# Two of four w_down blocks prepared from the copy that was loaded to measure them

## The chip, the cores and the metric

The kernel runs on one core of a Trainium2 chip. The core has five engines that each work through their own list of instructions in order and wait for one another by semaphores: TensorE (PE; its weight loads are shown as PEld), VectorE (DVE), ScalarE (ACT), GpSimd (POOL) and SyncE (SP). Here every DMA is issued by SP, so SP's list is also the order in which transfers start. The metric is the device time of one execution in microseconds.

## The reference

The input x has 4 batches of 2048 rows of 512 numbers. The block computes a cross-attention and then a feed-forward network whose operands are rounded to FP4 in blocks of 16:

```python
x = x + xattn(layernorm(x), ctx, ctx, mask, Wq, bq, Wk, bk, Wv, bv, Wo, bo)   # 16 heads of 32, 77 keys
x = x + ffn(layernorm(x), w_gate, w_up, w_down)

def fp4_quant_dequant(x):              # blocks of 16 along the last dimension
    scale = max(max(abs(block)) / 6, 1e-12)
    idx = searchsorted(MID, abs(block / scale))
    return GRID[idx] * sign(block) * scale

gate = fp4(x) @ fp4(w_gate).T          # w_gate, w_up: 1408 x 512
y    = fp4(x) @ fp4(w_up).T
h    = silu(gate) * y
out  = fp4(h) @ fp4(w_down).T          # w_down: 512 x 1408
```

So the three feed-forward weights have to be quantized and transposed on the chip before the first tile can use them. The kernel holds each quantized weight as two 16-bit parts (a high and a low one) with a common power of two, and that power comes from the largest absolute value of the whole matrix.

## The kernel before

The 8192 rows of x are worked through in 64 tiles of 128 rows. For a tile t the steps are: load x (xin), layernorm, transposition by DMA (xT), the product with Wq (qps), transposition (qst), scores (scps), maximum on DVE (mx), its negative on POOL (nmx), exponentials on ACT (line 944), the split into two parts (ph), transposition (pT), the product with the values (avps), normalization (an, ahl), transposition (aT), the product with Wo (ops), the residual sum (x, line 1004), the second layernorm, quantization and transposition (xqT), gate and up products (gps, ups), silu and product (hh), quantization (hqhl), transposition (hT), the down product (dps) and the store. Several tiles are in flight at once, so each engine's list interleaves steps of neighbouring tiles.

**The order of issue is written out.** Each piece of work is a Python generator that yields `step(engine, take, give, wait, fire)` and then emits its instructions. `take` and `give` name buffers of a ring (a buffer that is taken must have been given back by an earlier holder), `wait` and `fire` name events. The class Order (line 113) goes through a written list, INTRO (line 26), in which a word such as `wd0*2` means "two steps of the chain wd0"; then through 3013 steps that are chosen by the due times in PLACE (line 88), and last through OUTRO. Take, give, wait and fire don't make the chip wait: they only say which orders are allowed. What waits on the chip follows from the order of the instructions and the semaphores between them.

**The weights.** Before the first tile can go through the network, the kernel prepares w_gate, w_up and w_down in four blocks each. A block of w_down is 128 rows of 1408 numbers, 704 KB. Two functions deal with it:

- `down_max` (line 746; the word `ad` in INTRO) loads a block (tile name wmraw) into one of two buffers and takes the largest absolute value of every 16 numbers on DVE (wamd, line 377). Blocks 0 and 2 use the buffer hT, blocks 1 and 3 the buffer hqhl; both have one copy. The buffer is given back after the maximum, so the four blocks go 0, 1, 2, 3, two at a time. Then `weight_scale(2)` finds the largest value of the matrix.
- `weight_put(2, i)` (line 787; the words `wd0` to `wd3`) prepares block i. Its steps are: the reciprocal of the scales on DVE (rh, lines 763 and 764); a second load of the block into the same kind of buffer (tile name wraw); a multiply on POOL (line 704); the absolute value on ACT (wa, line 810); the rounding, two instructions on DVE (lines 710 and 711); the spread of the two parts of the scales on ACT (line 715, twice, from shh and slh, which `weight_scales`, line 775 and the words `sd`, makes); a multiply on DVE (line 719); and a DMA transposition into wdT (line 822), after which the buffer is given back.

So w_down is loaded twice. The second loads of blocks 0 and 1 are issued when the maxima are done, those of blocks 2 and 3 when block 0 has left hT and block 1 has left hqhl. The buffers hT and hqhl are later the ones that the down product of each tile uses, and `scales_h` (line 1053) waits until all four blocks are in wdT.

Other words of INTRO that matter below are `x.t` (residual, line 863: a load of x on SP, and the sum with the bias on POOL, line 869), `at.t` (attention, line 871), `kb` and `vb` (keys and values of the next batch).

Of the kernel before, what the change touches and what calls it, by code (L numbers as in the profile page):

```python
# [7 lines left out]
F32 = mybir.dt.float32  # L8
# [15 lines left out]
AHEAD = 14  # L24
PASSES = ((0, 0), (0, 1), (1, 0))
INTRO = (
    "lg*2 ck ag v wg0*3 ag sg lu au lu*3 wu0*3 au*2 wu2 au*4 wu1 wu3 au*3 wu2 wu0 wg0 o su*4 lk*6 mask wu1 lk ck*6 lk "
    "ck*3 lk*4 q*2 wu0 lg*2 ag*8 lo v lo v lo v lo*4 v*4 o*2 wu0 sg*2 ck*5 dc v q*4 wg2 su*2 lo o lo*2 o*2 wg0 su*2 "
    "sg at.0*3 pc0*4 dk pk1*2 v*3 dv pv2*2 pv1*2 pv2*2 pk1*2 at.1*3 pv0*2 wg0 wu2 wu1*2 pv3*2 pv1*2 lk q*2 dq pk3*3 "
    "wu0 wg2 at.0*3 at.2 wu2 pv0*2 pc1*2 wu1*2 pv3*2 pk3 pc1*2 pk0*2 sg*3 pk2*2 pc2*4 pk2*2 wg1 o*2 wg0 wu3 pk0*2 "  # L30
    "pq1*2 k pq3 kp pads pq3 pq1*2 pq3*2 o kp k*2 o*2 do mv wg3 su wu2 wu1 wg3 at.2 pq0*2 kp k kp k wu2*2 wg3*2 wg2 "
    "sg*2 pq2*2 at.2 at.1*3 at.3 pq0*2 vp mv vp mv pq2*2 po2 po0 po2*2 po0 po2 at.0 k*2 sg*3 wg3 wg2 wg3 k*4 wg2*2 "
    "wg1*2 wg3 wg2 ad wg1 po1*2 at.0*3 vp mv at.2*3 at.4 k*3 vp vp1 mv*2 vp2 vp3 x.0 wg1 at.3*2 po0*2 mv*5 vp2 vp3 "
    "vp1 ad sd ad wd0 po3*2 po1*2 vp3 wg1 k*2 at.3*2 at.5 at.1 at.3 at.1*2 ad wd1 ad keep po3*2 pads k*9 wu3 at.4 k*2 "
    "ad wd2 ad vp0 su*3 at.4*3 k0 at.5*2 vp0*2 v0*2 e0 v0*2 x.1*2 e0*2 v0 e0 v0 e0 v0*2 e0*2 v0 e0 ad wd0 ad*2 wd1 "
    "wu3 k0 f0 k0 f0 k0 f0 k0 f0 at.0*4 at.1 v0 e0 v0 e0 at.0 at.6*2 wg1 ad wd0*2 wd3 wd0 at.0 at.2 at.4 at.2*2 x.0 "
    "vp1 keep x.2 vp2 keep*2 x.3*2 ad*3 at.0*4 at.1 at.0 at.2 at.5*2 at.7 sd*3 wd0 at.1 at.0 at.1 wd0*2 wd2 at.0 wu3 "
    "at.7 wu3 at.3 at.5 sd*2 at.1*7 at.2 at.1 at.6 at.0*3 at.3*2 at.0 x.4 at.2*2 at.3 wd1*3 wd2*3 wu3 sd*2 at.6*2 "
    "at.8 at.2*2 wd1 sd wd2 sd*2 wd1*2 at.0 at.7 at.4 at.6 at.0*2 r.0 at.1*5 wd2*2 at.0*2 wd3 sd at.2*5 at.3 at.2 "
    "px.0*2 at.4*2 at.0*3 at.7*2 px.0 at.0 wd3*2 at.1 at.3 at.2 at.3*2 at.1*2 r.1 at.0 gu.0 at.8 at.9*2 at.1*2 x.2 "  # L40
    "at.3*3 at.2*2 at.4 at.5*2 at.7 wd3 gu.0*3 at.2*3 at.5 at.1 px.1*2 at.1 at.3*4 wd3*2 at.1*2 at.4 at.5 s.0 gu.0 "
    "h.0 gu.0 s.0 h.0 px.1 at.1*2 wd3 at.2*2 r.2 at.4 at.2*5 at.3*3 at.6 gu.1*2 at.4 px.2*3 at.4 at.3*3 at.2*3 s.0 "
    "gu.1 h.0 gu.1 h.0 ph.0*3 h.0 at.3*2 r.3 at.8 at.4*7 at.6*2 at.5 at.6 at.3*3 s.1 h.1 s.1 h.1 gu.2*4 at.5*2 ph.0*2 "
    "at.8*3 s.2 h.0*5 h.2 at.4*2 at.3*3 px.3*2 at.5*8 at.7*3 px.3 at.3 at.10 at.4*3 gu.1*2 s.1 h.1*4 at.3 s.2 h.2 h.1 "
    "at.6*2 at.7 at.6*7 x.4 ph.1*5 h.1 h.0*3 at.10 at.5 at.4*4 r.4 at.6*2 at.5*4 at.4*3 at.9 x.5 gu.2*2 s.2 h.2 "
    "at.8*3 h.1*2 gu.3 s.3 at.9 at.7*6 at.8 px.4*3 at.9*2 at.11 h.2 ph.2 h.2*2 gu.3 h.3 gu.3*2 at.6*4 at.4*4 ph.2 "
    "at.5 at.6 at.7*5 s.3 h.3 h.2 ph.2*2 x.5 at.5*3 h.2 h.1*3 r.5 at.11 at.5*3 at.10 x.6 gu.3 s.3 gu.3 h.3 at.9*3 "
    "ph.2 h.2*2 gu.4 s.4 at.10 at.8*6 at.9 px.5*3 at.10*2 at.12 h.3 ph.3 h.3*2 gu.4 h.4 gu.4*2 at.7*4 at.5*4 ph.3 "
    "at.6 at.7 at.8*5 s.4 h.4 h.3 ph.3*2 x.6 at.6*3 h.3 h.2*3 vb.16*2 r.6 at.12 at.6*3 at.11 x.7 gu.4*2 s.4 h.4 "
    "at.10*3 ph.3 h.3*2 gu.5 s.5 at.11 at.9*6 at.10 px.6*3 at.11*2 at.13 h.4 ph.4 h.4*2 gu.5*2 h.5 gu.5 at.8*4 at.6*4 "  # L50
    "ph.4 at.7 at.8 at.9*5 s.5 h.5 h.4 ph.4*2 x.7 at.7*3 h.4 h.3*3 r.7 at.13 ph.4 h.4 at.7*3 at.12 x.8 gu.5*2 s.5 h.5 "
    "at.11*3 gu.6 s.6 at.12 h.4 at.10*6 at.11 px.7*3 at.12*2 at.14 h.5 ph.5 h.5*2 gu.6*2 h.6 gu.6 at.9*4 at.7*4 ph.5 "
# [1 line left out]
    "at.12*3 gu.7 s.7 at.13 at.11*6 at.12 px.8*3 at.13*2 at.15 h.6 ph.6 h.6*2 gu.7*2 h.7 gu.7 at.10*4 at.8*4 ph.6 "  # L54
    "at.9 at.10 at.11*5 s.7 h.7 h.6 ph.6*3 x.9 at.9*3 h.6*2 h.5 h.6 h.5*2 r.9 at.15 at.9*3 at.14 x.10 gu.7*2 s.7 h.7 "
    "at.13*3 gu.8 s.8 at.14 at.12*6 at.13 px.9*3 at.14*2 at.16 h.7*2 ph.7 h.7 gu.8*2 h.8 gu.8 at.11*4 at.9*4 ph.7 "
    "at.10 at.11 at.12*5 kb.16*2 s.8 h.8 h.7 ph.7*3 x.10 at.10*3 h.7*2 h.6*2 h.7 h.6 r.10 at.16 at.10*3 at.15 x.11 "
    "gu.8*2 s.8 h.8 at.14*3 gu.9 s.9 at.15 at.13*6 at.14 px.10*3 at.15*2 at.17 h.8 ph.8 h.8*2 gu.9*2 h.9 gu.9 at.12*4 "
    "at.10*4 ph.8 at.11 at.12 at.13*5 s.9 h.9 h.8 ph.8*3 x.11 at.11*3 h.8*2 h.7*2 h.8 h.7 r.11 at.17 at.11*3 at.16 "
    "x.12 gu.9*2 s.9 h.9 at.15*3 gu.10 s.10 at.16 at.14*6 at.15 px.11*3 at.16*2 at.18 vb.16*12 h.9*2 ph.9 h.9 gu.10*2 "  # L60
    "h.10 gu.10 at.13*4 at.11*4 ph.9 at.12 at.13 at.14*5 s.10 h.10 h.9 ph.9*3 x.12 at.12*3 h.9*2 h.8*2 h.9 h.8 r.12 "
    "at.18 vb.16*10 at.12*3 at.17 x.13 gu.10*2 s.10 h.10 at.16*3 gu.11 s.11 at.17 at.15*6 at.16 px.12*3 at.17*2 at.19 "
    "h.10*2 ph.10 h.10 gu.11*2 h.11 gu.11 at.14*4 at.12*4 ph.10 at.13 at.14 at.15*5 s.11 h.11 h.10 ph.10*3 x.13 "
    "at.13*3 h.10*2 h.9*2 h.10 h.9 r.13 at.19 at.13*3 at.18 x.14 gu.11*2 s.11 h.11 at.17*3 vb.16*2 gu.12 s.12 at.18 "
    "at.16*6 at.17 px.13*3 at.18*2 at.20 h.11*2 ph.11 h.11 gu.12*2 h.12 gu.12 at.15*4 at.13*4 ph.11 at.14 at.15 "
# [20 lines left out]
    "h.63 ph.63*3 h.63*2 h.62*2 h.63 h.62 h.63*3 "  # L86
)
PLACE = dict(
    at=(1.3410, 2.1996, 3.3225, 3.5167, 3.5839, 3.3244, 4.3560, 0.1472, 1.9744, 4.1479, 5.5385, -2.2154, 4.8578,
        -2.6246, -10.7697, 4.2508, 5.9358, 4.9023, 1.4418, -0.6587, -0.5662, 6.8749, 6.3568, -1.2242, 6.4460,  # L90
        6.7669, 7.9337, 4.3122, 6.3881, -1.5407, 8.2952, 8.0546, 0.8043, 8.9161, -0.4174, 0.2812, 8.1137,),
    x=(7.3299, 8.0685,),
    r=(8.1990,),
    px=(8.5433, -3.1957, 6.1828,),
    gu=(9.4814, 9.8120, 2.3803, 9.6969, 10.3363, 0.6933,),
    s=(-6.3490, 10.0076, 8.3509,),
    h=(7.8032, 6.0659, 10.0005, 10.7935, 3.0743, 7.9790, 11.0188, 11.1705, -2.7181, 7.5435, 12.1737, 6.8093,
        12.1556,),
    ph=(5.4808, 10.9288, 11.0362, 2.0922, -3.0688,),
    kb=(1.9361, -4.2574,),  # L100
    vb=(-6.3353, -11.5998, 3.6216, -13.2874, 1.2251, 0.5808, -3.4649, 3.7683, -13.7683, -8.8449, -4.2453,
        -1.5424, -10.8163, -0.7213, 4.2224, -2.4971, -2.6961, -9.0082, -9.8222, -1.2915, 2.0183, -6.1307,
        4.1022, -6.2652, -19.8919, -9.7429,),
)


def step(e, take=(), give=(), wait=(), fire=(), on=False):


    return e, take, give, wait, fire, on  # L110
# [63 lines left out]
def tile_xattn_fp4_ffn(  # L174
# [19 lines left out]
    NB, S, D = x.shape  # L194
# [532 lines left out]
    def block_max(t, j, i):  # L727
        amax(wam[j][:, i], t.rearrange(blocks, j=Q))
# [15 lines left out]
        yield from weight_scale(j)  # L744

    def down_max():
        for i in range(G):
            tag = ("hT", "hqhl")[i % 2]
            yield step("D", take=[(tag, ("wd", i))], wait=[("mul", 1, 3), "mval"] if i == 0 else [])
            t = weight_load(buf(tag, [FF], F32, "wmraw"), 2, i)  # L750
            yield step("V", give=[(tag, ("wd", i))], fire=[("am", 2, i)])
            block_max(t, 2, i)
        yield from weight_scale(2)

    def block_scale(am, n, name):
# [31 lines left out]
    def weight_put(j, i):  # L787
        wk_ = ("wsm", ("w", j, i))
        yield step("V", wait=[("am", j, i)], take=[wk_])
        ri = reciprocals(wam[j][:, i], NH, "h")  # L790
        if j == 2:
            tag = ("hT", "hqhl")[i % 2]
            key = (tag, ("wp", i))
            yield step("D", take=[key], wait=[("am", 2, 2), ("am", 2, 3)])
            src = weight_load(buf(tag, [FF], F32, "wraw"), 2, i)
        else:
            src = parts[j, i]
        ak = ("ah", ("w", j, i))
        if j == 2:
            yield step("G", give=[wk_])  # L800
            t = src
        else:
            tag = scratch[(2 * j + i) % 4]
            key = (tag, ("w", j, i))
            yield step("G", take=[key], give=[wk_], wait=["mval"] if tag == "hqhl" else [], fire=[("mul", j, i)])
            t = buf(tag, [FF], F32, "wsc")
        normed(t, src, ri, NH)
        yield step("A", take=[ak])
        a = buf("ah", [FF], BF, "wa")
        nc.scalar.activation(a, t, AF.Abs, scale=RND)  # L810
        yield step("V")
        rounded(t, a)
        hl = t.bitcast(F16).rearrange("p (a d) -> p a d", a=2)
        yield step("A", wait=[("ws", j, i)], give=[("wss", (j, i))])
        sh, sl = tiles.pop(("ws", j, i))
        spread(hl, 0, sh, NH)
        spread(hl, 1, sl, NH)
        yield step("V", give=[ak])
        scaled(hl, a)
        if j == 2:  # L820
            yield step("D", give=[key], fire=[("wT", j, i)], wait=["kd", ("vals", 0)] + [("vd", b) for b in range(1, NB)])
            nc.sync.dma_start_transpose(out=wdT[:, :, i * P : (i + 1) * P], in_=flat(hl))
        else:
            w = [("mul", j, i // 2), ("mul", j, 2 + i // 2)]
            yield step("D", give=[key], fire=[("wT", j, i)], wait=w)
            for k in range(2):
                o = (wgT, wuT)[j][:, k * G + i].rearrange("p (i r) -> p i r", r=P)
                nc.sync.dma_start_transpose(out=o, in_=hl[:, k])
# [421 lines left out]
```

## Time and profile before

| what | us |
|---|---|
| median of 3 runs | 2003.44 (2000.14 to 2004.87) |
| the profiled execution | 2004.46 |
| its span, first to last instruction | 2002.7 |
| TensorE busy in the span | 1892.5 |
| VectorE busy | 1714.4 |
| ScalarE busy | 1385.5 |
| GpSimd busy | 917.0 |
| first loads of w_down (wmraw) issued | 101.4 to 122.1 |
| second loads of w_down (wraw) issued | 124.3 to 189.5 |

The page shows the span in 40 slices of 50 us; a digit is the busy share of an engine in tenths. A table by stretches gives busy time for each engine between two moments, and a chain of waits goes back from the last instruction to what released it at each step. A timeline has one line for each instruction or run of like instructions: start, duration, engine, line, operation, output and inputs, and in brackets how long the engine had been idle and what ended that. Instructions of SP are issues of DMAs: their duration is the time of issuing, not that of the transfer.

### The profile page before, as it was taken

How to read it: one execution, taken by the hardware profiler on the slowest of the kernel's cores; microseconds unless marked ns; L12 is line 12 of the kernel's file. 1: busy time of each engine (PE TensorE's matmuls, PEld its weight loads, DVE VectorE, ACT ScalarE, POOL GpSimd, SP SyncE). 2: the span in 40 equal slices, each digit the busy share in tenths (PEclk: the TensorE clock that was granted, in tenths of full speed). 3: DMA queues.
4: the chain of work that ended last, by engine and by line, in shares of the span. 5: the costliest groups of instructions: out<-in, count | busy, mean ns of one | idle time of the engine just before them, and what ended most of it. 6: DMA issues, size and time to landing. Idle time of an engine off the chain costs nothing.

```text
span 2002.7 us, 32553 instructions
## 1 busy us (share of the span) xinstructions
PE 1892.5 (94%) x11834; PEld 972.3 (49%) x11834; DVE 1714.4 (86%) x2810; ACT 1385.5 (69%) x2263; POOL 917.0 (46%) x1210
## 2 busy tenths in 40 slices
PE   2744999999999999999999999999999999999997
PEld 1622555555555555555555555555555555555543
DVE  7788988888888888898888888888889888888874
ACT  5867877667766777667766776677766776677531
POOL 4335345444444445544454445444454445444531
PEclk9866999999999999999999999999999999999999
DMA  8479676656656656665666575665765566656431
GB/s 251 91 198 206 105 136 127 130 120 125 133 121 131 122 122 125 132 120 121 129 129 118 123 130 119 132 126 116 135 131 114 120 128 128 119 117 114 88 76 45
DMA packets 778553, 252.80 MB, mean 126 GB/s; under 512 B 738292, under 2 KB 749684, under 8 KB 778391
## 3 DMA queue, kind: packets, MB, share of 16 engines
q1 hardware_dynamic: 778391, 250.72, 62.2%
q8 instruction: 92, 1.51, 0.3%
q14 instruction: 70, 0.57, 0.1%
HBM read 52.11 MB, written 17.92 MB: 35 GB/s over the span
## 4 chain that ended last, share of the span: by engine, by line
PE 88%; DVE 4%; ACT 3%; DMA 2%; POOL 1%; issue 1%; SPq 0%; DVEq 0%; POOLq 0%
PE dps L385 22%; PE gps L385 22%; PE ups L385 22%; PE ops L385 8%; PE qps L385 8%; PE avps L969 3%; PE scps L917 2%; PE wps L416 1%; ACT sc L944 1%; DMA hT<-hqhl 1%; DMA pT<-ph 1%; DMA wuT<-in_L_ffn_w_up_dram 0%; DVE wam L377 0%; DVE wsc L710 0%; DMA wdT<-wraw 0%
## 5 line engine op out<-in xcount | busy, mean ns | idle before, releaser
L385 PEld LDWEIGHTS <-xqT 128*128 128x128 f16 x4608 | 447.1, 98 | 453.9
L385 PE MATMUL ups<-wuT,xqT 128*128 128x512 f16 (+1 forms) x2304 | 487.8, 361 | 0.0
L385 PE MATMUL gps<-wgT,xqT 128*128 128x512 f16 (+1 forms) x2304 | 487.7, 361 | 0.0
L385 PE MATMUL dps<-wdT,hT 128*128 128x512 f16 x2112 | 468.4, 380 | 6.3 <-DMA hT<-hqhl 6.2
L944 ACT ACTIVATE sc<-sc,nmx,cells 128x77 f32<-128x77 f32 x1024 | 363.2, 438 | 8.6 <-POOL nmx L940 7.9
L385 PEld LDWEIGHTS <-hT 128*128 128x128 f16 x2112 | 206.8, 98 | 257.5 <-DMA hT<-hqhl 7.7
L1093 ACT ACTIVATE sg<-gps,cells 128x512 f32<-128x512 f32 (+1 forms) x192 | 123.8, 646 | 137.6 <-PE gps L385 133.0
L853 POOL TENSOR_SCALAR ve<-mv 128x1 f32<-128x1 f32 x128 | 111.1, 868 | 235.4 <-DVE mv L847 229.6
L385 PE MATMUL ops<-woT,aT 128*128 128x512 f16 x768 | 179.8, 384 | 17.3 <-DMA aT<-ahl 9.6
L704 POOL TENSOR_TENSOR hh<-hh,rh 128x1408 f32<-128x1408 f32 x64 | 165.7, 2589 | 42.8 <-DVE rh L764 42.3
L898 ACT ACTIVATE q<-qps 128x1024 f16<-128x1024 f32 x64 | 65.3, 1021 | 171.3 <-PE qps L385 171.3
L385 PE MATMUL qps<-wqT,xT 128*128 128x512 f16 x768 | 182.3, 389 | 0.0
L949 DVE TENSOR_TENSOR ph<-sc,ph 128x1232 f16<-128x1232 f32 x64 | 151.3, 2363 | 32.7 <-ACT ph L947 32.6
L883 ACT ACTIVATE xin<-xin,nb,rs 128x512 f32<-128x512 f32 x64 | 52.0, 813 | 173.5 <-POOL nb L881 173.5
L855 POOL TENSOR_TENSOR r<-ve,nhalf 128x1 f32<-128x1 f32 x128 | 153.5, 1199 | 10.7
L1103 DVE SCALAR_TENSOR_TENSOR hh<-ups,cells,sg 128x512 f32<-128x512 f32 (+1 forms) x192 | 128.5, 670 | 17.0 <-PE ups L385 15.3
L1069 POOL TENSOR_SCALAR cd<-pw,cells 128x1 f32<-128x1 f32 x64 | 18.3, 285 | 252.7 <-DVE pw L1066 252.7
L704 POOL TENSOR_TENSOR xc<-xc,rix 128x512 f32<-128x512 f32 x64 | 67.7, 1058 | 135.8 <-DVE rix L1020 130.3
L757 POOL TENSOR_SCALAR sh<-amh 128x88 f32<-128x88 f32 x64 | 33.3, 520 | 196.0 <-DVE amh L377 195.9
L385 PEld LDWEIGHTS <-xT 128*128 128x128 f16 x768 | 76.3, 100 | 87.5 <-issue 7.5
L385 PEld LDWEIGHTS <-aT 128*128 128x128 f16 x768 | 71.7, 99 | 96.6 <-DMA aT<-ahl 15.0
L857 POOL TENSOR_SCALAR e<-ve,r 128x1 f32<-128x1 f32 x128 | 102.7, 802 | 14.7
(190 smaller groups left out, 3023.3 us busy)
## 6 DMA issues: line engine op xcount, KB each, us to landing
xin<-in_x_dram SPq DMA_DIRECT2D x64, 256.0 KB
x<-in_x_dram SPq DMA_DIRECT2D x64, 256.0 KB
out_dram<-x SPq DMA_DIRECT2D x64, 256.0 KB
wgT<-in_L_ffn_w_gate_dram SPq DMA_DIRECT2D x4, 704.0 KB
wuT<-in_L_ffn_w_up_dram SPq DMA_DIRECT2D x4, 704.0 KB
wmraw<-in_L_ffn_w_down_dram SPq DMA_DIRECT2D x4, 704.0 KB
wraw<-in_L_ffn_w_down_dram SPq DMA_DIRECT2D x4, 704.0 KB
wqT<-in_L_xattn_Wk_dram SPq DMA_DIRECT2D x4, 256.0 KB
```

What stands on the lines that cost most here:

```text
L385: nc.tensor.matmul(o, lhs(a, c), rhs(b, c), start=(k == 0), stop=(k == 3 * n - 1))
L704: nc.gpsimd.tensor_tensor(dst.rearrange(blocks, j=Q), src.rearrange(blocks, j=Q), rinv.unsqueeze(2).to_broadcast([P, nb, Q]), ALU.mult)
L853: nc.gpsimd.tensor_scalar(ve, mv[:, 1:2], 1e-5, None, ALU.add)
L855: nc.gpsimd.tensor_tensor(r0, ve, nhalf, ALU.pow)
L857: nc.gpsimd.tensor_scalar(e, ve, r0, r0, ALU.mult, ALU.mult)
L883: nc.scalar.activation(xt, xt, AF.Identity, scale=rs, bias=nb_)
L898: nc.scalar.activation(q4[:, :, 0:3:2], q3.unsqueeze(2).to_broadcast([P, H, 2, DK]), AF.Copy)
L944: nc.scalar.activation(s3[:, h], s3[:, h], AF.Exp, scale=esc, bias=nm[:, h : h + 1])
L949: nc.vector.tensor_tensor(ph[:, 1, :SCW], sc, ph[:, 0, :SCW], ALU.subtract)
L969: nc.tensor.matmul(o[:, (lo - 8 * half_) * 33 : (hi + 1 - 8 * half_) * 33], pT[:rows, a * PC + c, :], vb[:rows, b_, c, (lo - CH0[c]) * 33 ...
L1093: nc.scalar.activation(sg, tiles.pop(("g", t, k)), AF.Silu, scale=cg[:, 0:1])
L1103: nc.vector.scalar_tensor_tensor(hh[:, c0 : c0 + n], tiles.pop(("u", t, k)), cg[:, 1:2], sg, ALU.mult, ALU.mult)
```

## The change

`down_max` takes the blocks in the order 2, 3, 0, 1. Blocks 2 and 3 give their buffers back after the maximum as before; blocks 0 and 1 keep theirs, and `weight_put` prepares them where they lie, without a second load. Blocks 2 and 3 are loaded a second time when block 0 has left hT and block 1 has left hqhl. INTRO and PLACE were written anew for this.

```diff
     def down_max():
-        for i in range(G):
+        for n, i in enumerate((2, 3, 0, 1)):
             tag = ("hT", "hqhl")[i % 2]
-            yield step("D", take=[(tag, ("wd", i))], wait=[("mul", 1, 3), "mval"] if i == 0 else [])
+            yield step("D", take=[(tag, ("wd", i))], wait=[("mul", 1, 3), "mval"] if n == 0 else [])
             t = weight_load(buf(tag, [FF], F32, "wmraw"), 2, i)
-            yield step("V", give=[(tag, ("wd", i))], fire=[("am", 2, i)])
+            yield step("V", give=[(tag, ("wd", i))] if n < 2 else [], fire=[("am", 2, i)])
             block_max(t, 2, i)
+            parts[2, i] = t
         yield from weight_scale(2)
...
         if j == 2:
             tag = ("hT", "hqhl")[i % 2]
-            key = (tag, ("wp", i))
-            yield step("D", take=[key], wait=[("am", 2, 2), ("am", 2, 3)])
-            src = weight_load(buf(tag, [FF], F32, "wraw"), 2, i)
+            key = (tag, ("wd" if i < 2 else "wp", i))
+            if i > 1:
+                yield step("D", take=[key], wait=[("am", 2, 0), ("am", 2, 1)])
+                parts[2, i] = weight_load(buf(tag, [FF], F32, "wraw"), 2, i)
+            src = parts[2, i]
```

What the new INTRO and PLACE make of the lists of instructions, compared engine by engine (tile names aside):

- SP: the two second loads of blocks 0 and 1 are gone. The load of x for tile 4 stands directly behind the second load of block 2; before, it stood behind xT, pT and aT that follow that load. One xin moves up by two places. At the start of each further batch the five loads of keys go ahead of an aT and a pT.
- POOL: before, the multiply of block 1 and that of block 2 stood in this order, then a sh (scales) and the nmx of tile 2. After, the sum x of tile 2 and the sh come first, then the multiply of block 2, then that of block 1, then nmx of tile 2. The sum x of tile 2 stood 25 instructions later before. Two memsets for the values go ahead of the constants of the first layernorm of an early tile.
- DVE: the pair rh of the last block to be prepared goes from before the rounding of block 0 to after the mx of tile 2. The rounding pairs of blocks 1 and 2 change places. The multiply (line 719) of the last block of w_up goes up behind that of block 0, and the sum x of tile 0 (line 1004) goes ahead of the multiply (line 719) of block 1.
- ACT: a shh goes ahead of the two wa of blocks 2 and 1, which change places; the spreads (line 715) keep the order block 1, block 2.
- PE: the same instructions in the same order, but for four small products of the preparation of Wq, Wk, Wv and Wo.
- In all, a few more neighbours change places early in the lists and at one tile in the network.

## The prediction

> **What bounds the kernel now.** I read the page's slices first, then the stretches, then the chain of waits up to 200 us, then single engines' timelines around the two places where w_down is reloaded.
>
> ```profile
> span 2002.7 us, 32553 instructions
> PE   2744999999999999999999999999999999999997
> DVE  7788988888888888898888888888889888888874
> ```
>
> ```profile
> 100.00:130.00 30.00, 15.53 (x108) 9.10 (x107) 25.14 (x44) 17.91 (x32) 15.09 (x30) 0.72 0.83 222
> 130.00:140.00 10.00, 8.22 (x48) 3.50 (x42) 6.52 (x7) 4.27 (x11) 3.81 (x4) 0.50 0.82 178
> ...
> 190.00:197.00 7.00, 4.97 (x13) 1.60 (x13) 6.90 (x11) 1.96 (x4) 2.29 (x1) 0.65 1.06 235
> 197.00:1950.00 1753.00, 1752.91 (x11007) 888.87 (x11008) 1538.26 (x2526) 1241.89 (x2021) 825.85 (x1089) 1.00 0.62 122
> ```
>
> (Columns: stretch, its length, busy us and count of PE, PE weight load, DVE, ACT, POOL; granted TensorE clock; DMA share; GB/s.) From 197 us TensorE is busy 1752.91 of 1753 us at the full clock. The change issues the same matmuls in the same order there, so **the time is the moment at which TensorE starts to run without gaps, plus a constant**. Whatever the edit does, it does by moving that moment, 196.98 us. Before it TensorE is mostly idle and the other engines prepare weights. The chain that leads there:
>
> ```profile
> 156.41 5.79 DMA wdT<-wraw
> 162.22 4.24 DMA wraw<-in_L_ffn_w_down_dram
> ...
> 166.61 2.59 POOL wraw L704
> ...
> 178.01 1.63 DVE wraw L719
> ...
> 190.11 6.83 DMA pT<-ph
> ...
> 196.98 1.34 PE avps L969 x33
> ```
>
> So a w_down reload is on it, the third one: block 2, which enters hT when block 0 has left it (wdT lands at 162.20, load issued 162.22). The other engines around it:
>
> ```profile
> 166.61 2.59 POOL L704 TENSOR_TENSOR wraw<-wraw,rh 128x1408 f32<-128x1408 f32 x1 [5.80 <-DVE sc L928]
> 171.16 2.78 POOL L940 TENSOR_SCALAR nmx<-mx,cells 128x16 f32<-128x16 f32 x1
> ...
> 168.24 2.44 DVE L710 SCALAR_TENSOR_TENSOR wraw<-wa,wraw 128x1408 f32<-128x1408 bf16 x1
> 172.26 1.62 DVE L710 SCALAR_TENSOR_TENSOR wraw<-wa,wraw 128x1408 f32<-128x1408 bf16 x1
> 178.01 1.63 DVE L719 TENSOR_TENSOR wraw<-wa,wraw 128x2816 f16<-128x2816 bf16 x1 [1.60 <-ACT wraw L715]
> ```
>
> The reader is to see that block 1's POOL multiply (158.22) was over long before, and that DVE worked on block 1 (168.24) while block 2 was still at POOL and ACT. From 179.70 to 190.11 SP issues back to back: wdT of block 1, xT, aT, wdT of block 2, the reload of block 3, pT of tile 2.
>
> **Part 1: the reloads of blocks 0 and 1 go** (issued 124.26 and 128.89; 704 KB each). The SP queue stood at the second until 128.89, since its buffer was still being read, but the next entry, qst of tile 0, waits for the scores that end at 133.0 and went out at 133.04: 0 on the path. Block 0's POOL multiply at 136.63 did not wait for its load either: it stands behind nmx (136.39), which waited for DVE's mx. That order is kept: 0. What is left is room on the DMA engines, busy 0.83 and 0.82 in these stretches. Two DVE waits there can shrink: 0.89 us for the fourth first load before 127.23, and 3.41 us for xin before 139.70. The next late thing is ACT's wa, which ends at 139.25 + 1.38 = 140.63.
>
> [...]
>
> **Part 2: one pair of rh (0.18 + 0.70 us) leaves DVE at 140.94** for a later place. With it, DVE's L710 on block 0 goes from 141.78 to about 140.95, 0.8 us sooner. Little of that passes: the next DVE ph (147.40) waits for ACT's ph, which ends at 145.67 + 1.23 = 146.90 whatever DVE does, so 0.5 us passes, to pT (148.90) and through SP's back-to-back entries to wdT of block 0 and the reload. I take **-0.5**, bounds -0.9 (the vd issues at 146.32 pass all of it on, and the 0.89 us is not added as ACT is next) and 0.
>
> **Part 3: blocks 1 and 2 change places on POOL, ACT and DVE.** Before: POOL block 1, wait, block 2, sh, nmx. After: x, sh (both long ready), wait, block 2, block 1, nmx. Let R be the start of block 2's multiply, 166.61 before. Before, DVE's L719 on block 1, which releases SP's run, ended at 179.64 = R + 13.0. After, POOL does block 2 until R + 2.6 and block 1 until R + 5.3 (2.59 each, 0.09 apart). ACT's wa of block 2 ends at R + 4.0, where DVE's L710 can start. It meets a POOL multiply still running, as at 168.24: there it ended 1.48 us after POOL's (169.20). So it ends at R + 6.75. Then L711 (1.63) and the pair for block 1 (1.62 + 1.65): R + 11.6. xhl and slh (0.97), x L1004, which now stands ahead (0.75): R + 13.3. L719 (1.63): R + 14.9. ACT is in time: wa of block 1 to R + 6.7, xin and xhl to R + 8.0, four exponentials (1.46) and two L715 (2.6) to R + 12.0. So **+1.9**. Low end +0.7, if L710 isn't held (1.2 less). High end +2.6: nmx of tile 2 waits on POOL behind block 1, took 2.78 us before, and if it gets in 3.2 us later (after the second pair) the L715 end near R + 14 and lead. Block 1's rh (Part 2) now stands after mx (166.88 + 1.44), 0.9 us that end before DVE gets the wa of block 2 at R + 4.0: 0.
>
> **Part 4: the load of x for tile 4 moves ahead on SP**, from 169.71 to directly behind block 2's reload, ahead of xT, pT and aT of the next tiles. Its 256 KB are 1.25 us at 206 GB/s (the stretch's rate). It is issued after the reload, as xT (162.60) and pT (164.19) were, and 4.24 us came out with those: I take **0**, bounds 0 and +1.25. The issue slot (0.58 us) only changes places; pT of tile 1 (164.19) waits for DVE's ph anyway, and avps of tile 1 is not on the path. POOL's add for tile 2 moves from 199.59 to about 158.3, where POOL then waits 5.8 us: 0; if that wait were gone, 1.27.
>
> **Part 5: the clock.** The last product before the start, ops of tile 1 (190.39), took 4.95 us, the same product after it 2.6: the clock was half and rose in between. If the start moves, the first group may fall in the half clock: 0 to +2.3; I take 0, since all of TensorE's bursts from 170 us move together. [...]
>
> **Part 6: other moves.** Two POOL memsets (0.48 apart) go ahead of tile 2's ve at 106.50, some early ACT and DVE neighbours swap, and on SP the batch's kst loads pass aT and pT three times (3.1 us of issue). aT issued at 432.26 is used at 453.57, so this has 18 us of cover; without it each boundary would cost up to 3. The memsets cost up to 0.2 in front of an ACT that waits for cells from DVE (108.07): 0.
>
> **Sum:** -0.5 + 1.9 = **+1.4 us**, with the bounds -0.2 and +6.2. The profiled execution took 2004.46 us, 1.8 more than its span, and is 1.0 above the median of the three runs, 2003.44; the shift is laid on the median: **2004.8 us**. 0.2% is 4.0 us, about what a measurement can tell here (the three runs spread over 4.7).
>
> **Rivals.**
> - *Slower: the late reload.* POOL now has block 2, block 1 and nmx behind one load, so its delay goes through in full. The longest 704 KB load in the chain took 8.65 us (wuT, 6.69), among queued loads; the others of w_down 5.2 to 5.6 (115.36, 122.06, 189.49). At 8.65 R is 4.4 later: 2003.4 + 1.4 + 4.4 = 2009.2. It decides from 6.9 us (+2.6). For it: DMA is at 0.90 to 1.06 from 150 us, with x now close behind. Against it: 4.24 with transposes behind.
> - *Faster: the DMA engines were the limit.* The two loads gone are 1.44 MB, 7.0 us at 205 GB/s. If all comes off everything after 130 us: 2003.4 + 1.9 - 7.0 = 1998.3; it decides from 5.9. Against it: a share of 0.82 and 0.65 in 130 to 150, and ACT's unbroken run to 146.90.
> - *Nothing moves*: both loads were hidden, and R comes 0.5 sooner while L710 isn't held, so SP's run starts within 0.2 of before: 2003.4.
>
> **How the numbers follow.** Forecast 0.50, nothing moves 0.12 (both within 0.2%); the slower one 0.25, since its waits add up on one queue; the faster one 0.13. So faster 0.13, same 0.62, slower 0.25. The forecast's own range is 2001.5 to 2008 (bounds, and a run's 1.5); the range reaches most of the way to the slower case and little to the faster: 2000.0 to 2009.0.
>
> **What would show it.** Block 0's L710 on DVE some 0.8 sooner; SP free between 124.7 and 133; POOL's two multiplies back to back at about 166 with nmx after; L719 of block 1 about 15 after R; SP's pT of tile 2 near 191.5 and avps near 198.4; nothing else from there. Wrong if R itself moves by more than 1, if pT is issued before 190, or if TensorE shows gaps after 200.

## The result, and the profile after

| | before | after |
|---|---|---|
| median | 2004.18 us (9 runs, 2000.14 to 2006.42) | 2010.23 us (9 runs, 2006.85 to 2014.83) |
| the profiled execution | 2004.46 us, span 2002.7 | 2011.79 us, span 2010.1 |

The ratio of the times is 1.0033, with a 95% interval of 1.0020 to 1.0046: the kernel became slower by 6.6 us (4.0 to 9.2). The forecast was 2004.8 us with a range up to 2009.0, so the result lies above the range, on the side to which 0.25 was given.

The slices of the kernel after look like those before: a start in which TensorE is mostly idle, then a full stretch.

```profile
span 2010.1 us, 32556 instructions
PE   2843999999999999999999999999999999999997
DVE  7778888888898888888888888888888888888874
```

The same stretches as before, with the start of the gapless part now at 200.88 us (columns: stretch, its length, busy us and count of PE, PE weight load, DVE, ACT and POOL; granted TensorE clock; DMA share; GB/s):

```profile
100.00:130.00 30.00, 13.09 (x86) 7.73 (x84) 23.30 (x43) 16.20 (x29) 11.00 (x29) 0.68 0.72 191
130.00:140.00 10.00, 7.94 (x61) 3.87 (x60) 7.15 (x6) 4.25 (x13) 5.46 (x4) 0.59 0.57 93
...
200.88:1950.00 1749.12, 1749.02 (x10971) 886.61 (x10972) 1535.19 (x2523) 1241.56 (x2020) 827.12 (x1088) 1.00 0.62 122
```

TensorE is busy for 1749.02 of 1749.12 us from there on: no gap has opened in the long part. The two spans differ by 7.4 us. Of these, 3.9 lie ahead of the start (196.98 and 200.88) and 3.5 behind it, of which 2.7 are the half clock of the first products (granted 0.50 from 200.88 to 206.48 us; Part 5 below); the 0.8 that is left is no more than this remainder varies by among the runs below (1805.1 to 1806.4 us where no half clock comes in). Ahead of the start DMA indeed has more room (0.72 and 0.57 where it was 0.83 and 0.82), to no use. The chain of waits of the kernel after shows the path through the start:

```profile
119.97 4.27 DMA wmraw<-in_L_ffn_w_down_dram
124.24 0.82 ACT xin L887
...
156.33 5.67 DMA wdT<-wmraw
162.02 4.24 DMA wraw<-in_L_ffn_w_down_dram
166.42 2.60 POOL wraw L705
...
181.81 1.62 DVE wmraw L720
...
193.83 7.01 DMA pT<-ph
200.88 2.27 PE avps L973 x33
```

One line of it needs care: ACT's xin is put down to the landing of the fourth load (wmraw, 119.97), which xin doesn't read. It reads nb from POOL, which ended at 124.20, as the timelines below show.

These are moments of two different executions, whose first loads were issued at different times (the first wmraw at 101.39 before, at 100.36 after; the fourth at 122.06 and 119.97). In the other runs below the time from the first to the fourth varies from 19.1 to 20.8 us without regard to the kernel. So the path is measured from the issue of the fourth first load. SP's lines for the moments that no chain shows, before and after (fourth first load, pT of tile 0, wdT of block 1):

```profile
122.06 0.36 SPq L268 DMA_DIRECT2D wmraw<-in_L_ffn_w_down_dram  x1
148.90 4.26 SPq L952 DMA_TRANSPOSE pT<-ph  x1
179.70 3.36 SPq L822 DMA_TRANSPOSE wdT<-wraw  x1
```

```profile
149.36 3.69 SPq L956 DMA_TRANSPOSE pT<-ph  x1
183.50 3.33 SPq L826 DMA_TRANSPOSE wdT<-wmraw  x1
```

| stretch of the path, us | before | after | difference |
|---|---|---|---|
| A: fourth first load issued, to reload of block 2 issued | 40.16 | 42.05 | +1.9 |
| of it, up to pT of tile 0 issued | 26.84 | 29.39 | +2.6 |
| B: reload of block 2, to wdT of block 1 issued | 17.48 | 21.48 | +4.0 |
| wdT of block 1, to avps of tile 2 | 17.28 | 17.38 | +0.1 |

The sum is +6.0 us, which is also the difference of the medians. Both large entries have a place on an engine.

**In A it is POOL.** The timeline of POOL, before (lines that were not shown yet):

```profile
109.81 0.55 POOL L757 TENSOR_SCALAR sh<-wamd 128x88 f32<-128x88 f32 x1 [0.93 <-DVE wamd L377]
...
111.61 2.26 POOL L757 TENSOR_SCALAR sh<-wam 128x88 f32<-128x88 f32 x1
...
122.39 0.27 POOL L881 TENSOR_SCALAR nb<-mv,rs 128x1 f32<-128x1 f32 x1
```

and after:

```profile
120.62 0.54 POOL L759 TENSOR_SCALAR sh<-wamd 128x88 f32<-128x88 f32 x1 [12.67 <-DVE wamd L378]
121.24 0.51 POOL L759 TENSOR_SCALAR sh<-wam 128x88 f32<-128x88 f32 x1
...
123.94 0.26 POOL L885 TENSOR_SCALAR nb<-mv,rs 128x1 f32<-128x1 f32 x1
```

and on DVE after, the maxima of block 0 and the xhl that waits:

```profile
118.91 1.62 DVE L378 TENSOR_REDUCE wamd<-wmraw 128x88 f32<-128x1408 f32 x1
...
125.75 0.69 DVE L891 TENSOR_TENSOR xhl<-xin,xhl 128x512 f16<-128x512 f32 x1 [3.25 <-ACT xhl L889]
```

The first `sh` of w_down, made from the maxima of block 0, stands at almost the same place in POOL's list in both: only memsets (one of ph, two of wdT) that stood behind it now go ahead of it. (In INTRO its word `sd` did move, from behind the first maximum to behind the third, because the step may not be issued before that maximum.) Before, block 0 was the first of the four loads, and its maxima were there after 0.93 us. Now block 0 is the third load (order 2, 3, 0, 1), its maxima end at 120.53, and POOL stands still for 12.67 us. Behind it in POOL's list are the last `sh` of w_up and the layernorm constants of tile 4 (ve to nb). So nb ends 4.2 us after the fourth load's issue, where it was 0.6; ACT's xin (124.24, in the chain above), DVE's xhl (125.75, idle for 3.25 us) and the chain up to tile 0's probabilities follow. The maximum of tile 0's scores ends 17.2 us after the fourth load's issue, where it was 14.2. That is 3.0 us lost; the 1.1 us by which A grew less were won behind it (Parts 1 and 2 below).

**In B it is the order of blocks 1 and 2.** Timelines of POOL, DVE and ACT after, around the reload:

```profile
166.42 2.59 POOL L705 TENSOR_TENSOR wraw<-wraw,rh 128x1408 f32<-128x1408 f32 x1 [5.46 <-DVE q L904]
170.12 2.58 POOL L705 TENSOR_TENSOR wmraw<-wmraw,rh 128x1408 f32<-128x1408 f32 x1 [1.12 <-DVE rh L766]
```

```profile
170.45 3.74 DVE L711 SCALAR_TENSOR_TENSOR wraw<-wa,wraw 128x1408 f32<-128x1408 bf16 x1 [0.40 <-ACT wa L814]
...
177.48 1.62 DVE L712 SCALAR_TENSOR_TENSOR wa<-wa,wmraw 128x1408 bf16<-128x1408 bf16 x1
...
181.81 1.62 DVE L720 TENSOR_TENSOR wmraw<-wa,wmraw 128x2816 f16<-128x2816 bf16 x1 [1.22 <-ACT wmraw L716]
```

```profile
179.14 1.38 ACT L716 ACTIVATE wmraw<-shh 128x1408 f16<-128x1408 bf16 x1 [2.28 <-DVE wa L712]
```

Two things are to be seen beside the swap itself. POOL's multiply on block 1 waits 1.12 us for `rh`, which now stands behind mx on DVE. And ACT's spreads of block 1 wait 2.28 us for DVE's second rounding instruction of block 1: they write into the buffer that this pair has to have read, and the pair now runs behind that of block 2. DVE's L720, which releases SP's run, waits for the spreads in its turn.

### The profile page after: what moved, and what is told of

It reads as the page before. It is cut to its first block, busy times and chain, and to the rows that moved or that the text cites. A ratio compares the mean times of both kernels' runs of the same rounds, so it can differ in the third digit from the quotient of the medians.

```text
span 2010.1 us, 32556 instructions
## 1 busy us (share of the span) xinstructions
PE 1891.8 (94%) x11834; PEld 972.3 (48%) x11834; DVE 1715.0 (85%) x2810; ACT 1385.5 (69%) x2263; POOL 917.4 (46%) x1210
## 4 chain that ended last, share of the span: by engine, by line
PE 87%; DVE 5%; ACT 3%; DMA 3%; POOL 1%; issue 1%; SPq 0%; DVEq 0%; POOLq 0%
PE dps L386 22%; PE gps L386 22%; PE ups L386 22%; PE ops L386 8%; PE qps L386 8%; PE avps L973 3%; PE scps L921 2%; ACT sc L948 1%; DMA hT<-hqhl 1%; DMA pT<-ph 1%; PE wps L417 1%; DVE wa L712 0%; DMA wmraw<-in_L_ffn_w_down_dram 0%; DMA wuT<-in_L_ffn_w_up_dram 0%; DVE wsc L711 0%
## 5 line engine op out<-in xcount | busy, mean ns | idle before, releaser
L386 PEld LDWEIGHTS <-aT 128*128 128x128 f16 x768 | 71.5, 98 | 97.8 <-DMA aT<-ahl 17.2
```

Of the source, the lines that this page charges most:

```text
L386: nc.tensor.matmul(o, lhs(a, c), rhs(b, c), start=(k == 0), stop=(k == 3 * n - 1))
```

## The experiments

In the diffs of INTRO each line is one word of the list, which stands for one step unless a number follows.

**1. Block 1 ahead of block 2 again.** The first theory (A) laid the whole loss on the swapped blocks.

```diff
...
 ad
-wd3
 ad
...
 ad
+wd1
 ad*2
...
 sd*2
-wd2
-wd1
-wd2*2
 wd1*3
+wd2*3
+wd3
 wu3
...
```

(The wd1 that moves up is its rh, the wd3 that moves down is block 3's.)

> The changed kernel with only the places of the steps of blocks 1, 2 and 3 altered: rh of block 1 directly after its maximum, rh of block 3 later, and the multiply, wa and rounding of block 1 ahead of those of block 2, as in the kernel before. The two loads stay removed, x of tile 4 stays ahead. Theory A (the order of blocks 1 and 2 is what costs, the removed loads are worth nothing): L720 on block 1 ends near R + 14 (R: start of the POOL multiply of block 2, about 166.4), SP starts its run of transpositions near 180.3 instead of 183.5, avps of tile 2 near 197.6 instead of 200.9, and the time is 3 to 6 us below the changed kernel, within 1.5 us of the kernel before (2004). Rival B (something else in the new order costs: the load of x for tile 4, the early swaps, or the steady order of SP): the time stays within 1.5 us of the changed kernel (2010).

Measured: 2008.88 us, ratio to the kernel before 1.0019 (1.0010 to 1.0028). B falls from 21.48 to 18.65 us, but A is 42.40, as in the kernel after. So the order of blocks 1 and 2, with the place of block 1's rh, was a cause, and not the only one: Theory A fell.

**2. The swap alone, in the kernel before.**

```diff
...
 at.3
+wd2*3
 wd1*3
-wd2*3
 wu3
...
```

> The kernel before, with all four reloads, and one swap in the written list: the POOL multiply, the wa and the rounding of block 2 ahead of those of block 1. Theory A: slower than before although nothing is removed: POOL does block 2 at R = 166.6 and block 1 after it, the spreads of block 1 wait for its rounding pair, L719 on block 1 ends near R + 16 (R + 13.0 before), SP starts its run near 182.6 (179.7 before), avps of tile 2 near 199.9 (197.0): +2.9 us, and up to +2.6 more where the clock falls badly: 2007 to 2009.5. Rival B: within 1.5 us of before (2004).

Measured: 2006.05 us, ratio 1.0007 (0.9998 to 1.0017). In the trace B becomes 20.63 us, +3.15; A stays at 40.27. The times are smaller than was expected, and by themselves don't tell this kernel from the one before; +3.3 us is just inside the interval's upper end (3.4). The trace shows the price of the swap: 3.2 us. In it, as in the kernel after, the rounding of block 2 is held by POOL's second multiply (it ends at 172.25, 1.48 us after the multiply's 170.77), and the multiply on DVE waits for the spreads:

```profile
169.67 2.58 DVE L710 SCALAR_TENSOR_TENSOR wraw<-wa,wraw 128x1408 f32<-128x1408 bf16 x1 [2.24 <-ACT wa L810]
...
179.81 1.66 DVE L719 TENSOR_TENSOR wraw<-wa,wraw 128x2816 f16<-128x2816 bf16 x1 [1.83 <-ACT wraw L715]
```

**3. TensorE kept busy.** The profiled execution after had its first group after the start at half the clock (granted 0.50 from 200.88 to 206.48 us). Here TensorE computes 20 products of 128x512 that nobody reads ahead of ops of tile 1, and 24 of 128x264 into the tile that avps of tile 2 then overwrites.

```diff
...
+            if t == 2 and half_ == 0:
+                for _ in range(24):
+                    nc.tensor.matmul(o, woT[:, 0, :P], woT[:, 0, : 8 * 33], start=True, stop=True)
...
+        if t == 1:
+            warm = ps.tile([P, 512], F32, tag="gu", name="warm", bufs=4)
+            for _ in range(20):
+                nc.tensor.matmul(warm, woT[:, 0, :P], woT[:, 0, :], start=True, stop=True)
         o = pmm(D, "ops")
...
```

> The changed kernel with extra matmuls that keep TensorE busy in two waits just before its start: 20 of 128x512 ahead of ops of tile 1, 24 of 128x264 ahead of avps of tile 2 (results unused). Theory C (part of the loss is the granted clock: avps 2.27 and the first gps 4.49 us in the changed kernel, 1.33 and 2.75 before): avps about 1.3, gps about 2.7, and the time 1.3 to 2.6 us below the changed kernel, 2007.5 to 2009. Rival (the clock is chance of one execution and plays no part in the median, or the extra work delays the real one): within 1 us of the changed kernel, or slower.

Measured: 2010.0 us, ratio 1.0027 (1.0017 to 1.0036). Avps of tile 2 takes 1.34 us and the next gps 2.76, as in the kernel before, where the granted clock was 1.00, and still the median is that of the kernel after. By the ratios it is 1.2 us less, with intervals that are 4 to 5 us wide. So the clock isn't shown to be a part of the loss in the medians; that it is one of a microsecond or two is not excluded.

**4. The load of x for tile 4 put back.**

```diff
...
-x.4
 wu3*2
...
 at.0
+x.4
 at.2*2
...
```

> The changed kernel with the load of x for tile 4 back in its old place, behind pT of tile 1 and aT of tile 0. Theory A: no difference, the reload of block 2 lands 4.2 us after its issue in both: within 1 us of the changed kernel (2010). Rival (the load close behind the reload holds it or pT up): R earlier by up to 1.25 us and the time lower by as much or more.

Measured: 2012.2 us, ratio 1.0036 (1.0023 to 1.0050), B 21.51. No cost of the load that stands closer is seen.

With these four, A was still unexplained: it was 42.0 to 42.5 in every kernel with the new order of loads, 40.2 in those with the old one. The wait of POOL on its first `sh` was the only new long one there, which made Theory D.

**5. The first sh moved behind what it held up.**

```diff
...
 ad*2
-sd
 wd0
 su*3
 at.4*3
+sd
 k0
...
```

> The kernel after, with one operation moved: POOL's first sh of w_down (scales of block 0) is issued behind su's last sh and the ve...nb group of tile 4 instead of ahead of them. Theory D (the wait of POOL for block 0's maximum, 12.67 us in the profile after, costs the time between the fourth first load and pT of tile 0): from the fourth issue of wmraw to pT of tile 0 takes 26.9 us again instead of 29.4, xhl on DVE no longer waits 3.25 us, and the median falls by about 2.6 us against the kernel after (about 2007.5). Rival (that stretch is set by the transfers or by the scores, not by POOL): the stretch stays at 29.4 and the time at 2010.

Measured: 2006.76 us, ratio 1.0014 (1.0006 to 1.0023). The timeline of POOL:

```profile
109.76 0.54 POOL L759 TENSOR_SCALAR sh<-wam 128x88 f32<-128x88 f32 x1
119.79 0.23 POOL L857 TENSOR_SCALAR ve<-mv 128x1 f32<-128x1 f32 x1 [9.49 <-DVE mv L851]
...
123.33 0.53 POOL L759 TENSOR_SCALAR sh<-wamd 128x88 f32<-128x88 f32 x1
```

The `sh` of w_up now runs at 109.76, ve no longer waits for block 0's maxima, and the `sh` of w_down waits for nothing. The fourth first load to pT of tile 0 takes 26.04 us instead of 29.39, a little more than the 2.6 that was expected; A is 38.98. The rival (29.4, 2010) is out. One word in the list was worth 3.1 us of A and, by the two ratios, 3.8 us.

**6. The same wait put into the kernel before.**

```diff
+    def late():
+        yield step("G", wait=[("am", 2, 2)])
+        s = sm.tile([P, NH], F32, tag="late", name="late", bufs=1)
+        nc.gpsimd.tensor_scalar(s, wam[2][:, 2], 1.0 / 6.0, 1e-12, ALU.mult, ALU.max)
...
 ad
+late
 vp0
 su*3
...
```

> The kernel before, with one more POOL operation, whose result is not used (1/6 of the maxima of block 2 of w_down, which is the third first load there): it stands where the kernel after has its first sh, ahead of su's last sh and tile 4's ve...nb, and makes POOL wait for the third maximum. Theory D: fourth first load to pT of tile 0 goes from 26.8 to about 29.4 us and the time rises by 2.6 us plus 0.5 for the operation at most (2006.5 to 2007.5). Rival: no change (2004.2).

Measured: 2008.91 us, ratio 1.0027 (1.0018 to 1.0035). POOL:

```profile
120.69 0.53 POOL L763 TENSOR_SCALAR late<-wamd 128x88 f32<-128x88 f32 x1 [11.54 <-DVE wamd L377]
...
122.34 0.50 POOL L757 TENSOR_SCALAR sh<-wam 128x88 f32<-128x88 f32 x1
...
125.04 0.27 POOL L886 TENSOR_SCALAR nb<-mv,rs 128x1 f32<-128x1 f32 x1
```

The wait appears (11.54 us), nb ends 5.3 us after the fourth load's issue, and A grows by 4.3 us, B by 0.2. It cost more than expected (5.4 by the ratio against 2.6 to 3.1), because two memsets stand between the wait and `sh` here and the chain of nb starts 1.1 us later than in the kernel after. The mechanism is shown from both sides.

**7. Both losses undone.** The `sh` moved as in 5, block 1 ahead of block 2 as in 1, with its rh in a wait of DVE.

```diff
...
 ad
-wd3
 ad
...
 ad*2
-sd
 wd0
 su*3
 at.4*3
+sd
...
 at.0*4
+wd1
 at.1
...
 sd*2
-wd2
-wd1
-wd2*2
 wd1*3
+wd2*3
 wu3
...
 wd1
+wd3
 wd1
...
```

> The kernel after, with the first scales moved as in the run before, and with block 1 of w_down taken ahead of block 2 on POOL, ACT and DVE (its rh in the idle time of DVE behind the maximum of tile 0's scores; block 3's rh behind block 1's scaling). If the two losses named (2.6 us before pT of tile 0, 4.0 us between the reload of block 2 and wdT of block 1) are all: within 1.5 us of the kernel before (2003 to 2005.5), with 26.9 us and 17.5 us in the two stretches. Rival (there is a third loss): still 2 us or more above before, with both stretches as before.

Measured: 2003.97 us, ratio 0.9999 (0.9990 to 1.0008). A is 39.15, B 18.22. The loss is gone to within 1.6 us (the upper end), so no third term of more than that is left in the time. The two stretches are not each as before: A is 1.0 us shorter (Parts 1 and 2 below) and B 0.7 longer, since DVE's L720 on block 1 now stands behind the sum x of tile 0, which waits 1.41 us for ops and takes 0.75.

**8. Block 1's rh alone put back early**, block 2 still first: this splits B's 4.0 us.

```diff
...
 ad
-wd3
 ad
...
 at.0*4
+wd1
 at.1
...
 wd2
-wd1
 wd2*2
...
 wd1
+wd3
 wd1
...
```

> The kernel after, with block 1's rh alone put back to an early place (in DVE's idle time behind the maximum of tile 0's scores; block 3's rh behind block 1's scaling): block 2 still goes ahead of block 1. POOL's multiply of block 1 then follows block 2's without the wait of 1.12 us, the held rounding of block 2 ends about 1 us sooner, and the stretch from the reload of block 2 to wdT of block 1 falls from 21.5 to 20.4 us; the time falls by about 1 us at most (2009). If rh was all of that loss, the stretch falls to 18 us; if rh was harmless, it stays at 21.5.

Measured: 2010.48 us, ratio 1.0024 (1.0013 to 1.0036); in time not to be told from the kernel after. In the trace, POOL and DVE:

```profile
168.66 2.82 POOL L705 TENSOR_TENSOR wraw<-wraw,rh 128x1408 f32<-128x1408 f32 x1 [4.28 <-DMA wraw<-in_L_ffn_w_down_dram]
171.44 2.59 POOL L705 TENSOR_TENSOR wmraw<-wmraw,rh 128x1408 f32<-128x1408 f32 x1
```

```profile
172.92 2.58 DVE L711 SCALAR_TENSOR_TENSOR wraw<-wa,wraw 128x1408 f32<-128x1408 bf16 x1 [0.34 <-ACT wa L814]
...
183.13 1.62 DVE L720 TENSOR_TENSOR wmraw<-wa,wmraw 128x2816 f16<-128x2816 bf16 x1 [1.22 <-ACT wmraw L716]
```

The two multiplies stand back to back, and B is 20.71: rh was 0.8 us of it. What remains, 3.2, is as much as the swap cost in the kernel before (experiment 2), and the wait of 1.22 us for the spreads is still there.

**9 and 10. Looking for a version that beats both.** Starting from experiment 7, the work on block 0 was taken earlier on POOL, ACT and DVE:

```diff
...
 k0
 f0
+wd0
 at.0*4
-wd1
...
 e0
+wd0*2
+wd1
 at.0
 at.6*2
 wg1
 ad
-wd0*3
...
 sd
+wd1
 sd
-wd1
...
```

> The kernel of the run with both losses undone, and block 0's POOL multiply moved ahead of tile 0's nmx (into POOL's idle time from about 133 us), its wa ahead of tile 0's exponentials on ACT, its rounding pair ahead of tile 6's first moments on DVE (idle there from about 137 us). If ACT's unbroken run up to ph of tile 0 sets pT of tile 0, that comes up to 2.4 us sooner, the reload of block 2 with it, and the time is 1 to 2.4 us below the kernel before (2002 to 2003). Rival: the start moves, but what follows the reload (pT of tile 2 waits for exponentials) eats it: 2004.

Measured: 2005.36 us, ratio 1.0001 (0.9992 to 1.0009); A 39.97, B 17.65. Nothing was won: POOL's multiply (128.99 to 132.96, 3.97 us instead of 2.59) fell on the rounding of the last block of w_up on DVE, whose second instruction took 3.89 us instead of 1.62 and ended 1.48 us after POOL's multiply. The maximum of tile 0's scores then ended 16.5 us after the fourth first load's issue (13.9 in experiment 7), and that is more than ACT had gained.

Then the work between the reload and the start was put in another order:

```diff
...
+wd1
 at.0
-wd1
-wd3
...
+at.2
 at.0
+at.2*2
...
+wd2
 at.1*2
+at.0*2
+wd2
 at.1*2
-wd2*2
-at.0*2
-wd3
-at.2*3
 at.2*2
+wd3
 at.3
 at.2
+wd3
...
-wd3*2
...
 at.3
+wd3
...
 at.3
+wd3
...
```

> The kernel with both losses undone, and the work between the reload of block 2 and TensorE's start put in another order: the scaling of blocks 1 and 2 on DVE ahead of what waits for TensorE's products, the exponentials of tile 2 on ACT ahead of the rest, on SP wdT of block 2 ahead of aT, and the reload of block 3 behind pT of tile 2 (its POOL multiply behind nmx of tile 3). Working from the profile of that kernel: wdT of block 1 issued about 2 us sooner, pT of tile 2 some 3 us sooner, so avps of tile 2 about 3 us sooner. If that start plus a constant is the time, the median is 2 to 3 us below the kernel before (about 2001). Rival: the late reload of block 3 opens a gap on TensorE behind the start, and the time is as before or longer.

Measured: 2003.25 us, ratio 0.9995 (0.9986 to 1.0004): not to be told from the kernel before. A is 38.87 and B 17.03, and TensorE reaches avps of tile 2 at 73.02 us after the fourth first load (74.92 before). But the next product is then late:

```profile
191.21 1.33 PE L973 MATMUL avps<-vblk,pT 128*128 128x66 f16 x33
194.00 2.77 PE L386 MATMUL gps<-wgT,xqT 128*128 128x512 f16 x12 [1.46 <-DMA xqT<-xqhl]
```

TensorE waits 1.46 us for xqT of tile 0, whose transposition SP issues behind pT. Counted to gps, the start is 0.3 us earlier than before (75.81 against 76.13). What follows the reload eats the gain, by another wait than the rival had named. No version was found that is measurably faster than the kernel before.

**All of them together.** A and B from each kernel's one profile, their sum against that of the kernel before (57.64), and what the times say (ratio less 1, times 2004 us, with its interval):

| kernel | A | B | A + B, shift | by the times |
|---|---|---|---|---|
| after | 42.05 | 21.48 | +5.9 | +6.6 (4.0 to 9.2) |
| 1 block 1 first | 42.40 | 18.65 | +3.4 | +3.8 (2.0 to 5.6) |
| 2 swap in before | 40.27 | 20.63 | +3.3 | +1.4 (-0.4 to 3.4) |
| 3 kept busy | 42.04 | 21.57 | +6.0 | +5.4 (3.4 to 7.2) |
| 4 x back | 42.53 | 21.51 | +6.4 | +7.2 (4.6 to 10.0) |
| 5 sh later | 38.98 | 21.37 | +2.7 | +2.8 (1.2 to 4.6) |
| 6 wait in before | 44.45 | 17.65 | +4.5 | +5.4 (3.6 to 7.0) |
| 7 both undone | 39.15 | 18.22 | -0.3 | -0.2 (-2.0 to 1.6) |
| 8 rh early | 42.13 | 20.71 | +5.2 | +4.8 (2.6 to 7.2) |
| 9 block 0 early | 39.97 | 17.65 | 0.0 | +0.2 (-1.6 to 1.8) |
| 10 start reordered | 38.87 | 17.03 | -1.7 | -1.0 (-2.8 to 0.8) |

Every shift lies within the interval of the times. These are 3.4 to 5.4 us wide, so the table is a coarse check, and the shift of experiment 10 leaves out the wait of 1.46 us behind its start. As far as the times can tell, the two stretches carry the differences of all eleven kernels.

## Why the prediction was wrong, point by point

- **What bounds the kernel** was right, to a few microseconds: the time is the moment at which TensorE starts to run without gaps, plus a constant. The constant (the span less the start of avps of tile 2) is 1805.1 to 1806.4 us in the five profiles whose first products ran at the full clock without a wait (before, experiments 2 to 5: avps 1.34 us, gps 2.76), and 1807.3 to 1809.2 in the other seven; in six of these avps and gps took longer (1.85 to 2.27 and 3.25 to 4.68 us), and in experiment 10 gps waited for xqT (1.46 us).
- **Part 1 (the two loads gone: 0)** held in its argument: block 0's multiply still stands behind nmx (137.31, then 137.56). (The entry that went out at 133.04 is qst of tile 1, whose place the scores of tile 0 had to leave; the time is read rightly.) But the path from pT of tile 0 to the reload of block 2 did become shorter, from 13.32 to 12.66 us (12.65 to 13.10 in the nine kernels with the new order of loads, 13.32 to 13.58 in the three with the old one), for which no part of the sum has a term. Which edit gives it was not separated.
- **Part 2 (rh leaves DVE: -0.5)** was right, and the trace shows it. DVE from the maximum of tile 0's scores to the rounding of block 0, before and after:

```profile
134.85 1.44 DVE L937 TENSOR_REDUCE mx<-sc 128x16 f32<-128x1232 f32 x1
139.70 0.69 DVE L845 BATCH_NORM_STATS2 st<-xin 128x6 f32<-128x512 f32 x1 [3.41 <-DMA xin<-in_x_dram]
...
141.78 1.56 DVE L710 SCALAR_TENSOR_TENSOR wraw<-wa,wraw 128x1408 f32<-128x1408 bf16 x1
```

```profile
135.78 1.44 DVE L941 TENSOR_REDUCE mx<-sc 128x16 f32<-128x1232 f32 x1
140.58 0.69 DVE L849 BATCH_NORM_STATS2 st<-xin 128x6 f32<-128x512 f32 x1 [3.36 <-DMA xin<-in_x_dram]
...
141.82 1.60 DVE L711 SCALAR_TENSOR_TENSOR wmraw<-wa,wmraw 128x1408 f32<-128x1408 bf16 x1
```

From st to the rounding it is 1.24 us instead of 2.08, and from the end of mx to the issue of pT 12.14 instead of 12.61. In the seven kernels with the new order that left this place alone (after, 1, 3, 4, 5, 7, 8) the latter is 12.14 or 12.15; in the three with the old one 12.55 to 12.66.
- **The step that failed outright is Part 6 (other moves: 0), which prices only instructions that change their place.** The `sh` of block 0 passed nothing but memsets on POOL, so a comparison of the lists shows nothing of weight there. What moved is the load that it waits for: block 0 went from first to third. Its wait grew from 0.93 to 12.67 us, and nb of tile 4 stands behind it. That is 3.1 us of A (experiment 5), and it is missing from the sum and from every rival.
- **Part 3 (the swap: +1.9, bounds +0.7 and +2.6)** had the right mechanism and the wrong size: +4.0. L711 of block 2 was held by POOL's multiply on block 1, as written, and it ended 1.49 us after it (1.48 was used). Two statements in it were wrong. That block 1's rh costs nothing, since it ends before DVE gets the wa of block 2, looked at DVE alone; POOL needs the rh and stood for 1.12 us (0.8 of B, experiment 8). And the spreads of block 1 were put at R + 12.0 as if they waited for ACT alone; they wait for block 1's rounding pair and ended at R + 15.4, which cost the 1.22 us of idle time ahead of L720. In the kernel before, this pair was done first, so that the dependency never showed as a wait. The 0.75 for the sum x of tile 0 was hidden behind that wait (the sum ended at 180.59, L720 began at 181.81); it shows in experiment 7, where the wait is gone.
- **Part 4 (x of tile 4: 0)** was right: the reload took 4.24 us from issue to landing, as before, and no gain is seen from putting the load back.
- **Part 5 (the clock: 0, up to +2.3)**: in the profiled execution avps and gps lost 0.94 + 1.73 = 2.7 us to the half clock (0.94 from 1.33 to 2.27, 1.73 from 2.76 to 4.49), a little over the bound, which came from one product (ops of tile 1, 4.95 us against 2.6); the granted clock was 0.50 for 6.82 us here, from 199.66 to 206.48 (see the last section). That execution is 1.6 above the median. What the clock does to the medians stays open within a microsecond or two (experiment 3).
- **The rivals.** The late reload was not it (4.24 us, decided from 6.9). The DMA engines as the limit were not it: they got their room, and of it the path can have used no more than the 0.7 us of Part 1. "Nothing moves" was not it. That the slower rival's 2009.2 came near the measured 2010.2, and that the upper bound of the sum, +6.2, covers the +6.0, is luck: the rival's late load didn't happen, and the bound gets there by terms for Part 4 and the clock, not by the wait on POOL.
- **The signs given for a wrong prediction misled.** R came at 166.42 (166.61 before), within the 1 us that was allowed, because in that execution the fourth first load was issued 2.1 us sooner by chance and hid the 1.9 us that A had lost. L719 (now L720) of block 1, at R + 17.0 instead of R + 14.9, and pT of tile 2, at 193.83 instead of 191.5, did show the error.

## What to carry to other kernels

When data are loaded in another order, go through the instructions that have *not* moved and ask of each which load it waits for now and what is queued behind it; a comparison of instruction lists is blind to this. When two chains change places on an engine, list every read and write of a buffer that the old order satisfied early, since none of them shows as a wait in the old trace. And compare two traces from an event on the path, not from the start of the span: here a chance shift of 2 us hid a loss of the same size.

## What the runs showed of the hardware

**A rounding instruction on DVE that met a POOL multiply ended about 1.5 us after it.** In five traces a rounding instruction of 128x1408 (two inputs; 1.62 us at the median in the kernel after) began before or during a multiply of 128x1408 on POOL and was still running when that ended. It ended 1.47 to 1.49 us after POOL's: 170.68 after 169.20 (before), 174.19 after 172.70 (after), 172.25 after 170.77 (experiment 2), 175.50 after 174.03 (experiment 8), 134.44 after 132.96 (experiment 9), for durations of 2.44, 3.74, 2.58, 2.58 and 3.89 us. In the kernel after the two overlapped for 2.25 us, and 1.49 of the usual 1.62 us still came behind POOL's end. In experiment 9 the instruction of DVE ahead of it had started first (128.35 to 130.52, 2.17 us long), and there POOL's multiply (from 128.99) ended 2.44 us after it, 3.97 us long instead of 2.59.

**The granted clock changed at moments that lie whole multiples of 3.41 us apart.** The kernel after, slices of 1 us (the clock is the third number from the end):

```profile
196.00:197.00 1.00, 1.00 (x5) 0.44 (x4) 1.00 (x3) 0.00 (x0) 0.00 (x0) 0.88 0.90 288
...
199.00:200.00 1.00, 0.00 (x0) 0.00 (x0) 0.97 (x3) 0.00 (x0) 1.00 (x1) 0.83 1.27 290
...
206.00:207.00 1.00, 1.00 (x5) 0.43 (x4) 1.00 (x1) 1.00 (x4) 0.00 (x0) 0.76 0.00 0
```

If 0.5 and 1.0 are its only levels (no other value lasts for more than one slice here), the means put the rise at 196.24, the fall at 199.66 and the next rise at 206.48: 3.42 and 6.82 us apart, one and two times 3.41. Read in the same way from slices of half a microsecond, the 22 changes between 100 and 210 us in the traces of before and after all lie whole multiples of 3.41 us from the next one in their trace, one to six of them. In the kernel after, TensorE was busy for 1.41 of the 3.42 us up to 199.66, and the clock fell to 0.5; it was busy for 2.2 us of the next 3.41, and the clock stayed there. In the kernel before, the clock rose at 194.88, TensorE was busy for 1.78 us of the next 3.42, and it kept the full clock. With the two traces cut into steps of 3.41 us at these moments, the 11 falls came after steps with 0 to 1.50 us of TensorE's work and the 11 rises after steps with 2.62 to 3.42; the rows give no sharp limit, since one step with 1.43 brought no fall and one with 2.99 no rise. An estimate from these rows, not shown by a run of its own: where the first product falls within a step decides over up to 2.7 us (the loss in the kernel after). Six of the twelve profiles have avps and gps of the start slower than at the full clock, and six don't. For one kernel the list of runs points the same way, though it doesn't show the cause: the kernel after took 2005.1 to 2006.6 us (span) in the four executions with a mean granted clock of 0.980, and 2008.5 to 2013.1 in the five with 0.976 to 0.978.
